# Edge products and one-hot matrices tile by tile in a graph-network kernel

## The chip, the cores and the metric

One core of a Trainium2 chip runs the kernel. The metric is the device time in microseconds (us), the median of several runs. The engines are PE (matrix products; PEld loads its weights), DVE (VectorE), ACT (ScalarE), POOL (GpSimd) and SP, which here only issues DMAs. Data lie in SBUF; PE's results arrive in PSUM.

## The reference

A graph network of three layers over 6250 nodes and 100000 edges, rows of 256 values, three relations. The edges are sorted by their destination. At the end the input is added and each row is normalised.

```python
def _gcn_forward(x, edge_index, edge_type, edge_attr, weights, roots, biases, edge_w, edge_b):
    n = x.shape[0]
    src, dst = (edge_index[0], edge_index[1])
    ew = edge_attr @ edge_w + edge_b
    rel_masks = [(edge_type == i).astype(x.dtype) for i in range(NUM_REL)]
    inv_cnt = [1.0 / jnp.maximum(jax.ops.segment_sum(m, dst, num_segments=n), 1.0) for m in rel_masks]
    for l in range(N_LAYERS):
        residual = x
        msg = jax.nn.relu(x[src] * ew)
        out = jnp.zeros((n, D), dtype=x.dtype)
        for i in range(NUM_REL):
            h = jax.ops.segment_sum(msg * rel_masks[i][:, None], dst, num_segments=n)
            h = h * inv_cnt[i][:, None]
            out = out + h @ weights[l, i]
        out = out + x @ roots[l] + biases[l]
        x = residual + jax.nn.relu(out)
    return x
...
x = _layernorm(x + _L0_gnn_ref(...), axis=-1)
```

## The kernel before

The edges stand in 782 tiles of 128, one edge to a partition, and two tiles make a pair: 391 pairs in each of three layers, 1173 in all. A setup turns the lists of sources, destinations and types into `src_i` (the source row of each edge) and `seg` (for each edge, its relation times 40 plus its destination counted from the first destination of its pair). A window of 40 destinations for each of three relations makes 120 columns (`WK`). During the setup POOL fills the small tile `limits` with hundreds of MEMSETs (L926), and DVE converts integers to floats (L902).

In the order in which the work of one pair depends on itself:

- `gather` (L575): POOL issues two indirect DMAs, one a tile, each of which fetches 128 rows of 256 floats from DRAM into its half of `xs[u]`, by the indices in one column of `src_i`. `xs` has 16 buffers, each of a pair.
- `weigh` (L612): DVE multiplies the pair's rows by the edge weights `ews`, in place. In layer 0 the weights are computed by PE (L589, L602), put into place by ACT (L609) and stored to DRAM; in layers 1 and 2 SP loads them again (L552).
- `bound` (L615): ACT applies the relu.
- `one_hot` (L619): DVE compares a row of the numbers 0 to 119 (`iota_w`) with each edge's `seg`; the result has a 1 in the column of the edge's relation and destination. In layer 0 ACT makes a bf16 copy (L623), from which the edges are counted.
- `reduce` (L629): PE multiplies rows by one-hots, and so adds up the pair's rows by relation and destination into `h_p` (PSUM).
- `add` (L645): DVE adds `h_p` to the window's place in `acc` (SBUF).

When all edges of a block of 128 nodes are in, PE multiplies its sums by the weights (`node_mul`, L673), DVE scales the three results and adds them to the root term (`node_end`, L704 and L705), and the new rows go to `x_mid` in DRAM, from which the next layer gathers; the next layer's first gather thus waits for the last rows. In the last layer ACT and DVE normalise the rows (L710 to L719), the last step by a TENSOR_SCALAR with two scalars a partition.

The order is written out by hand: one loop over steps (L741) issues at step `it` the gather of pair `it + 8`, the reduce of pair `it`, weigh and bound of pair `it + 3`, the add of pair `it - 1` (layer 0) or `it - 3`, what the root term and the nodes need, and last the one-hot of pair `it + 3`. Each engine works through its queue in that order. The two scalars of the change's one-hots and the gathers' indices are columns of `seg` and `src_i`, both in SBUF.

Of the kernel before, what the change touches and what calls it, by code (L numbers as in the profile page):

```python
# [12 lines left out]
ALU = mybir.AluOpType  # L13
# [429 lines left out]
def ordered_path(ctx, tc, x, edge_attr, weights, roots, biases, edge_w, edge_b, out, src_i, seg, place_i, consts):  # L443
# [4 lines left out]
    nc = tc.nc  # L448
    P = 128
# [11 lines left out]
    WK = R * WIN  # L461
# [10 lines left out]
    ident, ones, iota_w = consts  # L472
# [82 lines left out]
    def layer(l, r_sb, b_sb, ews, pools):  # L555
# [11 lines left out]
        xs, ew_ps, ats, ohs, h_ps, turns, o_ps, rs = {}, {}, {}, {}, {}, {}, {}, {}  # L567
# [41 lines left out]
                nc.scalar.activation(ews[q // 2][:, q % 2 * 2 + k], ew_ps[q][:, :, k, :], AF.Copy)  # L609

        def weigh(u):
            nc.vector.tensor_mul(xs[u], ews[u // 4][:, u % 4], xs[u])  # L612

        def bound(u):
            nc.scalar.activation(xs[u], xs[u], AF.Relu)  # L615

        def one_hot(u):
            ohs[u] = edge.tile([P, 2, WK], F32, name="oh", bufs=6)
            nc.vector.tensor_tensor(ohs[u], iota_w[:, None, :].to_broadcast([P, 2, WK]),  # L619
                                    seg[:, 2 * u:2 * u + 2, None].to_broadcast([P, 2, WK]), op=ALU.is_equal)  # L620
            if l == 0:
                oh_bs[u] = edge.tile([P, 2, WK], BF, name="oh_b", bufs=6)
                nc.scalar.activation(oh_bs[u], ohs[u], AF.Copy)  # L623
# [117 lines left out]
        for it in range(-9, max(starts) + 6):  # L741
# [21 lines left out]
            if pair(3) is not None:  # L763
                weigh(pair(3))
                bound(pair(3))
# [32 lines left out]
            if pair(3) is not None:  # L798
                one_hot(pair(3))
# [207 lines left out]
```

## Time and profile before

| | us |
|---|---|
| median of 3 runs | 3129.4 (3127.8 to 3131.9) |
| the profiled execution | 3133.5 |
| its span, first to last instruction | 3131.7 |
| DMA | 668 MB in 295322 packets, 213 GB/s mean |

The chain of work that ended last, by engine, as shares of the span:

```profile
PE 31%; DMA 21%; issue 19%; POOL 17%; DVE 9%; ACT 2%; DVEq 1%; POOLq 0%; ACTq 0%
```

A row of the groups of instructions names the line, the engine, the operation, the tiles, and in the longer form the shapes; then how often it ran, its busy time in us, the mean of one in ns, and the idle time of the engine just ahead of it with what ended it. Busy time of an engine leaves out the issuing of instructions between them. A row of a timeline has the start in us from the span's start, the duration in us, the engine, line, operation and tiles. A row of the windows has the stretch, its length, then busy time and number of instructions of PE, PEld, DVE, ACT and POOL, the granted clock of PE as a share of full speed, the share of time that the DMA engines were busy, and GB/s.

### The profile page before, as it was taken

To read this page: it belongs to the slowest core of one execution; us is meant where nothing else is said; L and a number is where in the kernel's file an instruction comes from. 1 tells how busy PE (TensorE), PEld (TensorE's weight loads), DVE (VectorE), ACT (ScalarE), POOL (GpSimd) and SP (SyncE) were. 2 spreads that over 40 slices of the span, in tenths; PEclk is the share of its full clock that TensorE was granted. 3 is DMA by queue.
4 is the path that set the end of the run, shared out by engine and by line. 5 is a ranking of instruction groups with operands and counts; after the bars stand their busy time and mean duration, and the time that the engine had idled before them with its cause. 6 is when DMAs were issued, how large, how long until landed. Compare 5 with 4: busy or idle time off the path is not lost.

```text
span 3131.7 us, 50860 instructions
## 1 busy us (share of the span) xinstructions
PE 2429.6 (78%) x14938; PEld 2108.6 (67%) x14938; DVE 2003.2 (64%) x4664; ACT 1302.0 (42%) x2524; POOL 2354.9 (75%) x3118
## 2 busy tenths in 40 slices
PE   4898999999998766677777777767677777877765
PEld 3777777778887666666666666656566666666665
DVE  4566666777776455566666666645566677777765
ACT  3666666666776422222333333222223333333332
POOL 7777777777777677777777777767777777777775
PEclk9899899999998778778888888766887888888886
DMA  4777776766776665656666666656666666666664
GB/s 135 233 233 231 222 241 213 228 216 217 230 231 213 217 218 199 213 200 218 205 217 205 221 221 217 206 184 223 211 208 223 220 217 209 224 228 216 218 216 138
DMA packets 295322, 668.14 MB, mean 213 GB/s; under 512 B 147224, under 2 KB 181996, under 8 KB 257788
## 3 DMA queue, kind: packets, MB, share of 16 engines
q1 hardware_dynamic: 175832, 350.27, 32.2%
q0 software_dynamic: 112608, 307.65, 31.6%
q10 hardware_dynamic: 6596, 6.87, 0.6%
q8 instruction: 124, 2.03, 0.3%
q14 instruction: 162, 1.33, 0.1%
HBM read 542.90 MB, written 121.70 MB: 212 GB/s over the span
## 4 chain that ended last, share of the span: by engine, by line
PE 31%; DMA 21%; issue 19%; POOL 17%; DVE 9%; ACT 2%; DVEq 1%; POOLq 0%; ACTq 0%
POOL xs L575 16%; PE h_p L629 15%; DMA xs<-x_mid,src_io 15%; PE o_p L673 7%; DMA xs<-in_x_dram,src_io 6%; PE ew_p L602 4%; DVE x_root L704 3%; DVE xs L612 2%; PE r_p L658 2%; DVE acc L645 2%; PE turn_p L589 1%; ACT ew_s L609 1%; POOL limits L926 1%; DVEq L645 1%; DVE oh L619 1%
## 5 line engine op out<-in xcount | busy, mean ns | idle before, releaser
L575 POOL DMA_INDIRECT xs<-x_mid,src_io x1564 | 1537.5, 983 | 509.0 <-issue 404.6
L629 PE MATMUL h_p<-oh,xs 128*128 128x120 f32 x9384 | 1451.6, 311 | 445.0 <-issue 177.8
L629 PEld LDWEIGHTS h_p<-oh,xs 128*128 128x128 f32 x9384 | 1364.3, 223 | 541.6 <-issue 309.4
L612 DVE TENSOR_TENSOR xs<-ew_s,xs 128x512 f32<-128x512 f32 x1173 | 808.0, 689 | 913.5 <-DMA xs<-x_mid,src_io 566.8
L615 ACT ACTIVATE xs<-xs 128x512 f32<-128x512 f32 x1173 | 739.5, 630 | 1484.9 <-DVE xs L612 1466.3
L575 POOL DMA_INDIRECT xs<-in_x_dram,src_io x782 | 789.6, 1010 | 247.1 <-issue 158.7
L645 DVE TENSOR_TENSOR acc<-h_p,acc 128x240 f32 (+1 forms) x1173 | 519.5, 443 | 147.0 <-PE h_p L629 74.7
L673 PE MATMUL o_p<-w_sb,acc 128*128 128x256 f32 (+1 forms) x1764 | 503.5, 428 | 89.2 <-DVE acc L645 52.1
L619 DVE TENSOR_TENSOR oh<-iota_w,seg_o 128x240 f32<-128x240 f32 x1173 | 467.0, 398 | 0.0
L673 PEld LDWEIGHTS o_p<-w_sb,acc 128*128 128x128 f32 (+1 forms) x1764 | 361.7, 216 | 152.4 <-DVE acc L645 57.6
L658 PE MATMUL r_p<-r_sb,t_s 128*128 128x256 f32 x588 | 216.3, 504 | 79.5 <-ACT t_s L654 78.8
L602 PE MATMUL ew_p<-ew_sb,at 33*128 33x256 f32 x1564 | 235.2, 421 | 10.9 <-ACT at L595 8.8
L609 ACT ACTIVATE ew_s<-ew_p 128x512 f32<-128x512 f32 x391 | 209.4, 587 | 41.5 <-PE ew_p L602 40.5
L704 DVE SCALAR_TENSOR_TENSOR x_root<-o_p,inv,x_root 128x256 f32<-128x256 f32 (+1 forms) x441 | 212.4, 482 | 20.9 <-PE o_p L673 8.6
L623 ACT ACTIVATE oh_b<-oh 128x240 bf16<-128x240 f32 x391 | 160.0, 409 | 117.9 <-DVE oh L619 111.0
L658 PEld LDWEIGHTS r_p<-r_sb,t_s 128*128 128x128 f32 x588 | 130.0, 245 | 111.3 <-ACT t_s L654 95.5
L602 PEld LDWEIGHTS ew_p<-ew_sb,at 33*128 33x128 f32 x1564 | 141.7, 195 | 44.8 <-ACT at L595 16.3
L690 ACT ACTIVATE acc<-zero_o 128x768 f32<-128x768 f32 (+1 forms) x150 | 141.0, 940 | 15.8 <-PE o_p L673 9.2
L629 PE MATMUL h_p<-oh_b,full_ones 128*128 128x120 bf16 x782 | 109.3, 223 | 0.0
L589 PE MATMUL turn_p<-ident_o,an 128*128 128x128 f32 x391 | 89.4, 312 | 7.9 <-DMA an<-in_edge_attr_dram 7.8
L589 PEld LDWEIGHTS turn_p<-ident_o,an 128*128 128x128 f32 x391 | 40.7, 145 | 77.1 <-issue 75.9
L650 PE MATMUL r_p<-ident_o,x_all 128*128 128x128 f32 x294 | 64.1, 303 | 30.9 <-DVE x_root L661 24.8
(84 smaller groups left out, 609.0 us busy)
## 6 DMA issues: line engine op xcount, KB each, us to landing
ew_s<-ew_all SPq DMA_DIRECT2D x194, 1024.0 KB
ew_all<-ew_s SPq DMA_DIRECT2D x97, 1024.0 KB
xs<-x_mid,src_io POOLq DMA_INDIRECT x1564
xs<-in_x_dram,src_io POOLq DMA_INDIRECT x782
an<-in_edge_attr_dram SPq DMA_DIRECT2D x97, 128.0 KB
x_mid<-x_all SPq DMA_DIRECT2D x96, 128.0 KB
x_all<-in_x_dram ACTq DMA_DIRECT2D x8, 768.0 KB
x<-in_x_dram SPq DMA_DIRECT2D x48, 128.0 KB
```

The lines of the kernel that those rows point to most:

```text
L575: nc.gpsimd.indirect_dma_start(out=xs[u][:, i, :], out_offset=None, in_=x_rows[:, :], in_offset=bass.IndirectOffsetOnAxis(ap=src_i[:, t:t ...
L589: nc.tensor.transpose(turns[q][:, k, :], ans[groups.index(q // 2) % 3][:, q % 2 * 2 + k].rearrange("p i a -> p (i a)"), ident)
L602: nc.tensor.matmul(ew_ps[q][:, i, k, :], ats[q][i * UP:i * UP + A1, k, :], ew_sb[i * UP:i * UP + A1, :], start=True, stop=True)
L609: nc.scalar.activation(ews[q // 2][:, q % 2 * 2 + k], ew_ps[q][:, :, k, :], AF.Copy)
L612: nc.vector.tensor_mul(xs[u], ews[u // 4][:, u % 4], xs[u])
L615: nc.scalar.activation(xs[u], xs[u], AF.Relu)
L619: nc.vector.tensor_tensor(ohs[u], iota_w[:, None, :].to_broadcast([P, 2, WK]), seg[:, 2 * u:2 * u + 2, None].to_broadcast([P, 2, WK]), op= ...
L629: nc.tensor.matmul(h_ps[u][:, d, :], xs[u][:, i, d * P:(d + 1) * P] if d < DC else full_ones, (ohs if d < DC else oh_bs)[u][:, i, :], star ...
L645: nc.vector.tensor_tensor(there, h_ps[u][:, :CH].rearrange("p c (r w) -> p c r w", r=R), there, op=ALU.add)
L658: nc.tensor.matmul(rs[c][:, 1, :], t_ss[c][:, d, :], r_sb[:, d, :], start=(d == 0), stop=(d == DC - 1))
L673: nc.tensor.matmul(o_p[:n, r, :], acc[:, d, r, slot:slot + n], w_sb[:, r * DC + d, :], start=(d == 0), stop=(d == DC - 1))
L704: nc.vector.scalar_tensor_tensor(root, o_p[:n, r, :], inv[:n, c, r:r + 1], root, op0=ALU.mult, op1=ALU.add)
```

## The change

The products of a pair, one instruction over both tiles, become one instruction for each tile. The one-hots of a pair, one comparison of two broadcast tensors, become for each tile one comparison of `iota_w` with a scalar for each partition, the edge's entry of `seg`. The order of the loop stays.

```diff
         def weigh(u):
-            nc.vector.tensor_mul(xs[u], ews[u // 4][:, u % 4], xs[u])
+            for i in range(2):
+                nc.vector.tensor_mul(xs[u][:, i, :], ews[u // 4][:, u % 4, i, :], xs[u][:, i, :])
...
         def one_hot(u):
             ohs[u] = edge.tile([P, 2, WK], F32, name="oh", bufs=6)
-            nc.vector.tensor_tensor(ohs[u], iota_w[:, None, :].to_broadcast([P, 2, WK]),
-                                    seg[:, 2 * u:2 * u + 2, None].to_broadcast([P, 2, WK]), op=ALU.is_equal)
+            for i in range(2):
+                nc.vector.tensor_scalar(ohs[u][:, i, :], iota_w, seg[:, 2 * u + i:2 * u + i + 1], None,
+                                        op0=ALU.is_equal)
```

On DVE's queue the first product of a pair now waits for the first tile's gather alone and the second for the second's; the two comparisons follow each other.

## The prediction

> **What bounds the kernel.** The page's first two rows come first: no engine is full.
>
> ```profile
> span 3131.7 us, 50860 instructions
> PE 2429.6 (78%) x14938; PEld 2108.6 (67%) x14938; DVE 2003.2 (64%) x4664; ACT 1302.0 (42%) x2524; POOL 2354.9 (75%) x3118
> ```
>
> POOL's 75% is misleading, as the groups show (busy, mean ns of one, then the idle time ahead of it and who ended it):
>
> ```profile
> L575 POOL DMA_INDIRECT xs<-x_mid,src_io x1564 | 1537.5, 983 | 509.0 <-issue 404.6 <-DMA x_mid<-x_all 32.8 <-PE h_p L629 25.0
> L575 POOL DMA_INDIRECT xs<-in_x_dram,src_io x782 | 789.6, 1010 | 247.1 <-issue 158.7 <-ACT oh_b L623 18.9 <-PE h_p L629 15.8
> L612 DVE TENSOR_TENSOR xs<-ew_s,xs 128x512 f32<-128x512 f32 x1173 | 808.0, 689 | 913.5 <-DMA xs<-x_mid,src_io 566.8
> L619 DVE TENSOR_TENSOR oh<-iota_w,seg_o 128x240 f32<-128x240 f32 x1173 | 467.0, 398 | 0.0
> ```
>
> Taken singly from the trace, the idle time ahead of a gather is 303 to 306 ns, except at the two layer boundaries. So POOL never waits for a buffer: gather follows gather, each at its own duration plus 304 ns. The windows, cut at the first and last gather of each layer, show the same (PE, PEld, DVE, ACT, POOL busy; granted clock; DMA):
>
> ```profile
> 38.30:1066.00 1027.70, 944.78 (x6819) 789.05 (x6819) 687.77 (x1515) 683.63 (x1467) 789.58 (x782) 0.94 0.72 226
> 1066.00:1082.10 16.10, 10.26 (x79) 8.84 (x75) 7.49 (x18) 4.94 (x9) 0.00 (x0) 0.97 0.64 225
> 1082.10:2087.60 1005.50, 719.52 (x3969) 641.55 (x3970) 605.49 (x1410) 296.35 (x493) 767.53 (x782) 0.81 0.63 212
> 2087.60:2104.10 16.50, 11.13 (x43) 9.24 (x41) 6.66 (x16) 2.10 (x3) 0.00 (x0) 0.62 0.12 34
> 2104.10:3112.40 1008.30, 729.85 (x3974) 649.21 (x3974) 674.05 (x1652) 306.74 (x542) 769.97 (x782) 0.80 0.64 215
> 3112.40:3131.70 19.30, 7.50 (x36) 6.43 (x36) 7.50 (x20) 2.29 (x4) 0.00 (x0) 0.76 0.06 18
> ```
>
> The three stages of 782 gathers take 3041.5 us of the span. The shortest gather is 942 ns: 2346 x (0.942 + 0.304) = 2923 us. The rest, 117 us, is gathers that ran longer. The change can only act there, in the three drains (52 us together), or by making another engine late.
>
> **Why gathers run long.** Median 946 ns, but 465 of 2346 take over 1000. The 412 that overlap no DVE instruction average 946, and one of them is long. Of the 465, 464 began while a DVE instruction with two SBUF inputs was running; additions that read PSUM (L645) don't do it. An example from the timeline (start, duration):
>
> ```profile
> 1647.40 0.69 DVE L612 TENSOR_TENSOR xs<-ew_s,xs 128x512 f32<-128x512 f32 x1
> 1647.58 1.33 POOL L575 DMA_INDIRECT xs<-x_mid,src_io  x1 [0.30 <-issue]
> ```
>
> L612 ends 0.51 us after the gather's start, and the gather is 0.39 us longer than 942 ns. Over all cases the excess is (end of the DVE instruction - start of the gather - about 145 ns). With a second such instruction queued right behind, the excess still follows the first one's end (90 cases of L619 before L612): the gather gets in between two instructions. By the instruction in the way, the 117 us are: L612 about 84, L619 22, L705 and others 4, and 7 of a few ns each.
>
> **Part 1, products in halves.** One of 689 ns becomes two of 256 elements; the nearest row is L663 (two SBUF inputs, 128x256), 414 ns. Consecutive DVE instructions overlap by 82 ns in the timeline, so a pair costs DVE 2 x 332 = 664 ns instead of 607: +57. For POOL each half is in the way until its own end alone. The longest excess falls from 689 - 145 = 544 to 414 - 145 = 269 ns, and with starts at random the sum goes with 2 x 269^2 against 544^2, a factor 0.49. Applying the rule to every recorded start of L612, but with two halves there, gives 41 us; moving all starts by -600 to +600 ns gives 41 to 75, mean 56. I take 48, between: **84 - 48 = 36 us saved**. The first half waits for the first gather alone, the second for the second, so the product ends no later.
>
> **Part 2, one-hots by a scalar.** One TENSOR_TENSOR of 240 becomes two TENSOR_SCALARs of 120 elements, one SBUF tensor each. What L619 cost POOL, **22 us**, goes. What a TENSOR_SCALAR costs POOL is the open point.
>
> Duration: L719 is the nearest row (128x256 f32, two scalars read from SBUF), 411 ns at least. Casts of 896 and 784 elements took 630 and 548 ns and one of 391 took 341: some 0.57 ns an element, about half the 1.07 of TENSOR_TENSOR ((689 - 414)/256). At half of 1.07, 120 elements take 411 - 136 x 0.54 = 338, less one scalar (54 ns: L704 with a scalar 482, L705 without 428): 284. At the full 1.07 it would be 265 with both scalars, so the ends lie close. DVE: 2 x (284 - 82) = 404 against 398 - 82 = 316, +88 a pair.
>
> Port: the Trainium skill, "SBUF — State Buffer", section "Who interferes with whom", speaks against this part: TENSOR_SCALAR in its double-rate mode takes the port pair that DVE shares with GpSimd for the whole instruction, and GpSimd, which writes the gathers' descriptors, is fully blocked; TENSOR_TENSOR only keeps GpSimd from reading. Start-up confirms it for POOL's MEMSETs, beside the CAST at 13.4 us and beside the TENSOR_TENSOR at 24.0 (durations min/median/max):
>
> ```profile
> L926 POOL MEMSET limits<- x12: 88/435/569, 13.3 to 13.7; 1x1 f32 x12
> ...
> L926 POOL MEMSET limits<- x17: 88/88/89, 24.0 to 24.5; 1x1 f32 x17
> ```
>
> Beside gathers the 49 L719s show something else: no gather was longer for one, while it was L719 that waited.
>
> ```profile
> 2244.25 0.98 POOL L575 DMA_INDIRECT xs<-x_mid,src_io  x1 [0.30 <-issue]
> 2244.83 0.51 DVE L719 TENSOR_SCALAR x_all<-x_all,mv 128x256 f32<-128x256 f32 x1
> ```
>
> L719s that start 0.49 to 0.60 us into an undelayed gather all end 1.06 us after its start (up to 572 ns instead of 411); those that start at 0.19 to 0.31 us aren't delayed. So a gather uses the pair for a short while some 0.6 to 0.8 us in, and in a shorter one at its start, where L719s beginning 0.1 us ahead lost 10 ns. But no L719 happened to hold the pair at the moment when a gather asked. By those rows a one-hot costs POOL 0. By the rule, it is in the way for all its 284 ns: at the write 284^2 / (2 x 1310 ns, the mean gather period) = 31 ns, at the read (284 - 145)^2 / 2620 = 7.4 ns, together 38 ns x 2346 = 90 us. I take the side of L719, but not its end, since nothing tested the collision: only the last 200 ns hold the pair and half of a delay is absorbed (200^2 / 2620 / 2 = 7.6 ns), plus 2 ns at the read: 9.4 ns x 2346 = **22 us back**.
>
> **Part 3, DVE.** +145 ns a pair; 1173 pairs, 170 us of DVE time, plus its waits for the pair. It hides under POOL: a pair takes POOL about 2.6 us, DVE 1.3 of per-pair work, about 1.45 afterwards, and the last stage's node work adds some 0.35. The 16 xs buffers are the cover: additions come 7 to 9 pairs behind the gathers, 11 at most. If the lag passed 16, every further DVE ns would be paid.
>
> **Drains.** The last products start on landings and the chain then runs through L629, L645, L673 and L704; 0 us, give or take 1 each.
>
> **Sum.** 3133.5 (profiled execution: 3131.7 span and 1.8 around it) - 36 - 22 + 22 = 3097.5. The median of the runs is 4.1 below that execution: **3093 us**, 36 below the median, 1.2%.
>
> **Rivals.**
> - **One-hots cost POOL nothing**: 3133.5 - 58 - 4 = 3071. For it: all 49 L719s. Against: the MEMSETs stalled by a CAST.
> - **One-hots lock GpSimd out (slower)**: the rule in full, 90 us: 3133.5 - 58 + 90 - 4 = 3162. For it: the MEMSET rows, and 2346 such instructions where there were 49. Against: L719s held the pair for much of the first 0.6 us without delaying a gather. It decides once a TENSOR_SCALAR costs POOL over 58/2346 = 25 ns.
> - **DVE becomes late in the last stage**: 674 of 1008 us busy already. If a pair needed 2.7 us there instead of 2.55, 391 x 0.15 = 59 us: about 3152. It needs 0.9 us a pair that I can't find.
>
> **Chances.** Forecast 0.52 (own range 3078 to 3112), one-hots free 0.20, lock-out 0.22, DVE late 0.04; 0.02 for none of these. A measurement of this kernel tells 0.2% (6 us) from no change. Faster: the first two less their upper spill, 0.70; within 0.2%: 0.07; slower 0.23. The range 3058 to 3165 takes in both bounds of the one-hot's price and the lower end of the halves' (41 us).
>
> **What the next profile would show.** Right: L575 still with 304 ns ahead of each, its mean about 977 (992 now over both rows), those that a product holds up at most 1.21 us instead of 1.47; the product's halves at 414; one-hots at 265 to 340. One-hots free: mean near 968. Lock-out: gathers that last until a one-hot's end, mean above 1000. Wrong altogether: POOL idle for a buffer, waiting for PE's L629, or halves that fall on gathers' starts more often than at random.

## The result, and the profile after

| | before | after |
|---|---|---|
| median of 17 runs each, us | 3130.98 (3126.41 to 3138.41) | 3122.41 (3115.45 to 3125.82) |
| ratio, 95% interval | | 0.9971 [0.9964, 0.9979] |
| profiled execution, us | 3133.5 | 3124.6 |
| its span, us | 3131.7 | 3122.8 |

The change makes the kernel 0.3% faster, 9 us. The forecast was 36 us. The page after, its first rows and the shares of the chain:

```profile
span 3122.8 us, 50763 instructions
PE 2404.4 (77%) x14938; PEld 2085.5 (67%) x14938; DVE 2188.1 (70%) x7010; ACT 1306.9 (42%) x2524; POOL 2349.3 (75%) x3118
...
DMA 26%; PE 26%; POOL 15%; issue 15%; DVE 13%; ACT 3%; DVEq 1%; POOLq 0%; ACTq 0%
```

DVE has 185 us more work, and POOL, whose gathers bound the kernel, only 6 us less. The groups (busy, mean ns, idle time ahead and what ended it):

```profile
L575 POOL DMA_INDIRECT xs<-x_mid,src_io x1564 | 1546.1, 989 | 505.6 <-issue 386.5 <-DMA x_mid<-x_all 29.5 <-PE h_p L631 29.0
...
L613 DVE TENSOR_TENSOR xs<-ew_s,xs 128x256 f32<-128x256 f32 x2346 | 910.6, 419 | 713.9 <-DMA xs<-x_mid,src_io 552.8 <-DMA xs<-in_x_dram,src_io 83.2 <-ACT ew_s L609 69.5
L575 POOL DMA_INDIRECT xs<-in_x_dram,src_io x782 | 775.4, 992 | 247.1 <-issue 139.6 <-PE h_p L631 18.9 <-ACT oh_b L625 17.7
...
L621 DVE TENSOR_SCALAR oh<-iota_w,seg_o 128x120 f32<-128x120 f32 x2346 | 588.3, 297 | 0.0
```

Over both gather rows the mean went from 992 to 990 ns, not to 977. In layers 1 and 2 (x_mid) it even rose, from 983 to 989; all of the gain stands in layer 0 (1010 to 992). The windows, cut as before, agree:

```profile
38.45:1050.80 1012.35, 935.43 (x6822) 779.32 (x6823) 746.12 (x2290) 684.74 (x1466) 774.31 (x782) 0.96 0.73 229
1050.80:1067.90 17.10, 9.78 (x74) 8.46 (x72) 8.72 (x25) 5.46 (x10) 1.05 (x1) 0.91 0.62 220
1067.90:2074.10 1006.20, 717.40 (x3966) 637.85 (x3966) 668.04 (x2183) 295.39 (x492) 768.13 (x782) 0.81 0.63 212
2074.10:2088.60 14.50, 8.29 (x44) 7.47 (x44) 8.18 (x25) 2.73 (x4) 1.03 (x2) 0.88 0.17 47
2088.60:3102.70 1014.10, 717.75 (x3972) 640.34 (x3973) 734.28 (x2429) 310.34 (x542) 776.05 (x782) 0.81 0.63 214
```

Layer 0 is 15.3 us shorter, layer 1 as long as before, layer 2 5.8 longer. The books close: the two gather rows hold 5.6 us less busy time and 3.4 us less idle time, the latter at the layer boundaries (29.5 against 32.8 us); that is the 8.9 us of the span.

So what a gather lasts beyond 942 ns is again the whole question: 111.5 us in sum, 117.2 before. Nearly every long gather can be put down to a DVE instruction, since it ends about 0.8 us after the end of the one it waited for: the prediction's 942 - 145 = 797 ns, and in the median some 22 ns more. Of the 465 long ones before, 2 waited beyond the instruction that was running at their start, for the end of a further one. After the change 66 of 498 did. The timeline shows one (start, duration; x2 joins two instructions that follow each other):

```profile
2630.94 0.46 DVE L621 TENSOR_SCALAR oh<-iota_w,seg_o 128x120 f32<-128x120 f32 x2
...
2631.32 0.75 DVE L613 TENSOR_TENSOR xs<-ew_s,xs 128x256 f32<-128x256 f32 x2
2631.49 1.40 POOL L575 DMA_INDIRECT xs<-x_mid,src_io  x1 [0.30 <-issue]
...
2632.31 0.62 DVE L621 TENSOR_SCALAR oh<-iota_w,seg_o 128x120 f32<-128x120 f32 x2
```

The first half of the product began at 2631.32 and, at 419 ns, ended at 2631.74; the second ended at 2632.07. Had the gather got in between, it would have lasted 1.04 us. It lasted 1.40: 2631.49 + 1.40 - 0.797 = 2632.09, the end of the second half. I call this **held through**. The last row is the other side: two one-hots took 0.62 us instead of 0.46 while a gather was 0.8 us into its work.

### The profile page after: what moved, and what is told of

Same layout as the page of the kernel before. It is cut to its first block, busy times and chain, and to the rows that moved or that the text cites. A ratio compares the mean times of both kernels' runs of the same rounds, so it can differ in the third digit from the quotient of the medians.

```text
span 3122.8 us, 50763 instructions
## 1 busy us (share of the span) xinstructions
PE 2404.4 (77%) x14938; PEld 2085.5 (67%) x14938; DVE 2188.1 (70%) x7010; ACT 1306.9 (42%) x2524; POOL 2349.3 (75%) x3118
## 4 chain that ended last, share of the span: by engine, by line
DMA 26%; PE 26%; POOL 15%; issue 15%; DVE 13%; ACT 3%; DVEq 1%; POOLq 0%; ACTq 0%
DMA xs<-x_mid,src_io 22%; POOL xs L575 14%; PE h_p L631 12%; PE o_p L675 7%; DMA xs<-in_x_dram,src_io 5%; DVE xs L613 4%; PE ew_p L602 4%; DVE x_root L706 3%; DVE acc L647 3%; PE r_p L660 2%; DVE oh L621 2%; ACT ew_s L609 1%; PE turn_p L589 1%; POOL limits L928 1%; ACT xs L616 1%
## 5 line engine op out<-in xcount | busy, mean ns | idle before, releaser
L631 PE MATMUL h_p<-oh,xs 128*128 128x120 f32 x9384 | 1434.0, 308 | 436.6 <-DVE acc L647 342.9
L631 PEld LDWEIGHTS h_p<-oh,xs 128*128 128x128 f32 x9384 | 1346.0, 220 | 533.9 <-issue 286.6
L613 DVE TENSOR_TENSOR xs<-ew_s,xs 128x256 f32<-128x256 f32 x2346 | 910.6, 419 | 713.9 <-DMA xs<-x_mid,src_io 552.8
L575 POOL DMA_INDIRECT xs<-in_x_dram,src_io x782 | 775.4, 992 | 247.1 <-issue 139.6
L621 DVE TENSOR_SCALAR oh<-iota_w,seg_o 128x120 f32<-128x120 f32 x2346 | 588.3, 297 | 0.0
L675 PE MATMUL o_p<-w_sb,acc 128*128 128x256 f32 (+1 forms) x1764 | 495.7, 423 | 86.9 <-DVE acc L647 50.3
L602 PE MATMUL ew_p<-ew_sb,at 33*128 33x256 f32 x1564 | 232.4, 417 | 13.0 <-ACT at L595 11.5
L692 ACT ACTIVATE acc<-zero_o 128x768 f32<-128x768 f32 (+1 forms) x150 | 141.0, 940 | 12.6 <-PE o_p L679 6.8
L631 PE MATMUL h_p<-oh_b,full_ones 128*128 128x120 bf16 x782 | 108.2, 221 | 0.0
```

Of the source, the lines that this page charges most:

```text
L575: nc.gpsimd.indirect_dma_start(out=xs[u][:, i, :], out_offset=None, in_=x_rows[:, :], in_offset=bass.IndirectOffsetOnAxis(ap=src_i[:, t:t ...
L602: nc.tensor.matmul(ew_ps[q][:, i, k, :], ats[q][i * UP:i * UP + A1, k, :], ew_sb[i * UP:i * UP + A1, :], start=True, stop=True)
L613: nc.vector.tensor_mul(xs[u][:, i, :], ews[u // 4][:, u % 4, i, :], xs[u][:, i, :])
L621: nc.vector.tensor_scalar(ohs[u][:, i, :], iota_w, seg[:, 2 * u + i:2 * u + i + 1], None, op0=ALU.is_equal)
L631: nc.tensor.matmul(h_ps[u][:, d, :], xs[u][:, i, d * P:(d + 1) * P] if d < DC else full_ones, (ohs if d < DC else oh_bs)[u][:, i, :], star ...
L675: nc.tensor.matmul(o_p[:n, r, :], acc[:, d, r, slot:slot + n], w_sb[:, r * DC + d, :], start=(d == 0), stop=(d == DC - 1))
```

## The experiments

All of them are read in the same sum, by what a long gather waited for. Each row is one profiled execution, in us, with the number of gathers; "others" is every other instruction and a few ns on the rest. A held gather's whole excess stands under "held through", also the part for the first instruction, and also where that was a one-hot. The ratio is to the kernel before on the same chip. Where a layer's code was the same, its excess still scattered by a few us: layer 0 had 53.0 in the kernel before and 50.9 and 58.1 in e11 and e12, and 36.0, 34.5 and 35.0 in e1, e9 and e10.

| kernel | product | held through | one-hot | others | excess | ratio to before, 95% |
|---|---|---|---|---|---|---|
| before | 82.7 (329) | 0.9 (2) | 21.8 (189) | 11.8 | 117.2 | 1 |
| after | 52.9 (390) | 33 (66) | 6.0 (111) | 19.6 | 111.5 | 0.9971 [0.9964, 0.9979] |
| e1 halves alone | 47.0 (423) | 3.4 (6) | 29.4 (268) | 14.9 | 94.7 | 0.9933 [0.9915, 0.9952] |
| e2 one-hots alone | 99.8 (471) | 20.6 (32) | 5.7 (112) | 11.5 | 137.6 | 1.007 [1.005, 1.0089] |
| e3 addition between | 68.8 (528) | 5.6 (11) | 4.4 (80) | 14.4 | 93.2 | 1.0041 [1.0022, 1.006] |
| e4 one-hot between | 79.7 (576) | 5.5 (12) | 6.4 (104) | 12.2 | 103.8 | 0.998 [0.9969, 0.999] |
| e5 TENSOR_TENSOR by tile | 56.1 (394) | 8.2 (15) | 27.6 (291) | 16.3 | 108.2 | 0.9982 [0.9974, 0.9991] |
| e6 the same, whole product | 97.4 (469) | 3.4 (5) | 18.1 (250) | 12.6 | 131.5 | 1.0033 [1.0021, 1.0045] |
| e7 one-hots ahead of addition | 51.0 (374) | 32 (59) | 7.6 (129) | 14.4 | 105.0 | 0.9973 [0.996, 0.9985] |
| e8 quarters | 19.0 (241) | 103 (231) | 11.0 (147) | 15.8 | 148.8 | 1.0133 [1.011, 1.0157] |
| e9 comparison from PSUM | 69.0 (424) | 8.8 (20) | 8.9 | 14.6 | 101.3 | 0.9973 [0.9959, 0.9988] |
| e10 the same from SBUF | 51.6 (378) | 24.2 (48) | 14.9 | 15.0 | 105.7 | 0.9966 [0.9953, 0.9979] |
| e11 e9 with whole product | 109.2 (445) | 1.1 | 7.3 | 12.0 | 129.6 | 1.0058 [1.0046, 1.0071] |
| e12 layers 1, 2 without one-hots | 106.7 (374) | 1.2 | 10.3 | 15.5 | 133.7 | 1.0043 [1.0031, 1.0055] |

### e1 and e2: each part by itself

e1 is the kernel before with the change's `weigh`; e2 is the changed kernel with the product of before.

```diff
 # e1, from before
-            nc.vector.tensor_mul(xs[u], ews[u // 4][:, u % 4], xs[u])
+            for i in range(2):
+                nc.vector.tensor_mul(xs[u][:, i, :], ews[u // 4][:, u % 4, i, :], xs[u][:, i, :])
 # e2, from after
-            for i in range(2):
-                nc.vector.tensor_mul(xs[u][:, i, :], ews[u // 4][:, u % 4, i, :], xs[u][:, i, :])
+            nc.vector.tensor_mul(xs[u], ews[u // 4][:, u % 4], xs[u])
```

> Products in halves, one-hots as before. Theory (gathers that wait behind a first half are often held through the second half too, so that halving saves next to nothing): the gathers' excess over 942 ns each stays at 105 to 117 us in all, 20 us of it from gathers held through both halves; time 3120 to 3131 against 3130 before. Rival (the scalar one-hots take the gain away): without them the 36 us of the prediction show, excess near 81, time near 3094.

> Products whole as before, one-hots by a scalar for each tile. Theory (a one-hot by a scalar costs the gathers about 8 us in all where the whole one-hot cost 22): excess near 103, time near 3116. Rival (the scalar one-hots lock GpSimd out): excess 117 or more, time 3130 or above.

e1 took 3107.4 us against 3127.0 for the kernel before on its chip: **0.9933**, the fastest version of all, faster than the change too. Its gather rows:

```profile
L575 POOL DMA_INDIRECT xs<-x_mid,src_io x1564 | 1532.0, 980 | 507.2 <-issue 376.3 <-DMA x_mid<-x_all 31.3 <-PE h_p L630 29.5
...
L575 POOL DMA_INDIRECT xs<-in_x_dram,src_io x782 | 772.7, 988 | 247.1 <-issue 136.5 <-ACT oh_b L624 21.7 <-PE h_p L630 20.1
```

Against the kernel before these hold 22.4 us less. Halves by themselves are not held through (6 gathers), so the time lies between the two expectations. The one-hot got dearer, 29.4 for 21.8 us (268 gathers for 189): some gathers that no longer met a product may have met a one-hot.

e2 is **slower** than before, 3150.6 us, though its one-hots cost gathers only 5.7 us:

```profile
L575 POOL DMA_INDIRECT xs<-x_mid,src_io x1564 | 1564.1, 1000 | 506.0 <-issue 401.6 <-DMA x_mid<-x_all 30.0 <-DMA xs<-x_mid,src_io 28.0
```

And its timeline (start, duration):

```profile
2466.39 0.47 DVE L620 TENSOR_SCALAR oh<-iota_w,seg_o 128x120 f32<-128x120 f32 x2
...
2466.62 1.66 POOL L575 DMA_INDIRECT xs<-x_mid,src_io  x1 [0.30 <-issue]
2466.77 0.69 DVE L612 TENSOR_TENSOR xs<-ew_s,xs 128x512 f32<-128x512 f32 x1
```

The lock-out of the forecast's slower rival would give gathers that end 797 ns after a one-hot. The timeline shows something else: this gather began during the one-hots, which were over at 2466.86, and lasted until 797 ns after 2467.48, where the product behind them ended (2467.46). Besides 32 such cases, 471 gathers waited for a product, 329 before. So a one-hot alone cost little, but the held gathers, too, had begun during one-hots: with their 20.6 us, one-hots and what followed them held up gathers for 26.3 us, and the plain waits for a product rose by 17.1 us besides.

### e3 and e4: something else between the halves

If a gather is held because the second half follows at once, an instruction that leaves gathers alone, put between, should let it in.

```diff
 # e3, from after: in the loop, ahead of and behind the addition
+                weigh(pair(3), 0)
...
+            if pair(3) is not None:
+                weigh(pair(3), 1)
+                bound(pair(3))
 # e4, from after: in weigh, after each half
+                nc.vector.tensor_scalar(ohs[u][:, i, :], iota_w, seg[:, 2 * u + i:2 * u + i + 1], None,
+                                        op0=ALU.is_equal)
```

> The changed kernel with the addition, which reads PSUM, set between the two halves of a product. Theory (held through both halves): no gather is held through two halves, 20 us go: excess near 90, time near 3101. Rival (the halves only meet more gathers' starts than at random): excess stays near 111, time near 3121.

> The changed kernel with each half of a product followed by one one-hot by a scalar, and the addition after both. Theory (a gather is held over where the next DVE instruction also uses the port pair that DVE shares with GpSimd): fewer gathers pass in between than with the addition, some are held through half, one-hot and half; excess 90 to 115, time 3100 to 3125. Rival (only two products in a row hold on): as with the addition, excess near 90, time near 3101.

Both let it in: 11 and 12 gathers held, for 66. A one-hot by a scalar between the halves thus served as well as the addition, against the theory of e4. But the halves, now apart, met more gathers (528 and 576 for 390), so a part of it came back as plain waits. e4 took 3122.1 us, as long as the change. e3 has the smallest excess of all, 93.2, and was still slower than the kernel before. The waits of POOL say why (us in total, times, longest):

```profile
POOL xs L575 <- issue: 551.6, 1781, 6.2
...
POOL xs L575 <- DMA x_mid<-x_all: 44.0, 2, 30.0
POOL xs L575 <- ACT xs L615: 22.5, 62, 1.7
```

In the changed kernel no wait of a gather is over 0.32 us but at the two layer boundaries. Here gathers waited up to 6.2 us inside layer 0, 17.6 us in all (264.7 idle for 247.1), and 30.0 us at the first boundary, 16.1 in the changed kernel. At the end of each of the nine waits over 0.9 us inside the layers, the reduces stood 14 or 15 pairs behind the gather, so that the pair 16 back had only just been read out of the buffer that the gather wanted; in the changed kernel they stood at most 9 behind. The 16 buffers of `xs` were used up. Around the longest wait:

```profile
767.29 0.53 DVE L646 TENSOR_TENSOR acc<-h_p,acc 128x360 f32 x1 [3.96 <-PE h_p L630]
767.74 0.41 DVE L612 TENSOR_TENSOR xs<-ew_s,xs 128x256 f32<-128x256 f32 x1
767.92 1.05 POOL L575 DMA_INDIRECT xs<-in_x_dram,src_io  x1 [6.15 <-issue]
```

The addition waited 3.96 us for PE, and the second half, which the relu and the next reduce need, came only after it. That this order used up the buffers is likely; it wasn't tested apart.

### e5 to e8: which instructions let a gather be held

```diff
 # e5, from after; e6 the same with the whole product
-                nc.vector.tensor_scalar(ohs[u][:, i, :], iota_w, seg[:, 2 * u + i:2 * u + i + 1], None,
-                                        op0=ALU.is_equal)
+                nc.vector.tensor_tensor(ohs[u][:, i, :], iota_w, seg[:, 2 * u + i:2 * u + i + 1].to_broadcast([P, WK]),
+                                        op=ALU.is_equal)
 # e7, from after: one_hot(pair(3)) moved ahead of add in the loop
 # e8, from e5
-                nc.vector.tensor_mul(xs[u][:, i, :], ews[u // 4][:, u % 4, i, :], xs[u][:, i, :])
+                for h in range(0, D, P):
+                    nc.vector.tensor_mul(xs[u][:, i, h:h + P], ews[u // 4][:, u % 4, i, h:h + P], xs[u][:, i, h:h + P])
```

> The changed kernel, its one-hots tile by tile still, but by a TENSOR_TENSOR with seg broadcast in place of the TENSOR_SCALAR: as many instructions of about the same duration (120 x 1.07 + 139 = 267 ns), without the scalar and without the port pair taken for writing. Theory (it is the TENSOR_SCALARs right ahead of the products behind which gathers are held through a further instruction): 5 or fewer gathers held through where the changed kernel has 64, products cost near 50 us, the one-hots 10 to 15, excess near 70, time 3080 to 3095. Rival (the number of instructions in a row does it, the mode doesn't matter): 40 or more held through, excess near 110, time near 3121.

> Products whole, one-hots tile by tile by TENSOR_TENSOR: against the run with one-hots by a scalar alone it differs in the mode only. Theory (mode): excess near 82 + 13 + 4 = 100, none held through, time near 3112. Rival (count): 30 or more held through a product as in that run, excess near 138, time near 3147.

> The changed kernel with the one-hots of a step moved ahead of its addition, so that an addition stands between the scalar one-hots and the next products. Theory (held through only where products follow the scalar one-hots directly): fewer than 15 gathers held through, excess near 80, time near 3092. Rival (where they stand doesn't matter): 50 or more held through, excess near 111, time near 3121.

> Products in quarters of 128 elements (276 ns each), one-hots tile by tile by TENSOR_TENSOR: the dose of the port rule. Theory (a gather waits for the end of one instruction only): a quarter is in the way for at most 276 - 145 = 131 ns, so products cost 25 us instead of 50, excess near 42, time near 3060. Rival (in a longer row of instructions gathers are held through): excess 80 or more, time 3090 or more.

e5 has the change's instructions in number and place, with TENSOR_TENSOR one-hots of 276 ns. Held gathers fell from 66 to 15, so the operation of the one-hots bears on whether a gather waiting for a product is held. The moment at which a gather starts doesn't explain it: of those that began 165 to 180 ns into a first half that had followed its predecessor at once, 27 of 50 were held in the changed kernel and 2 of 41 in e5. The time didn't fall (3126.2), since these one-hots delay gathers themselves: 27.6 us, not the 10 to 15 expected. e6 has hardly any held ones, yet its products cost 97.4 for 82.7 before and it took 3145.1 us, near its rival's time for another reason. e7 shows that the place of the one-hots isn't what matters: 59 held, and the change's time.

e8 settles that short instructions in a row are no remedy. A quarter of a product takes 287 ns, and the cost of single waits fell to 19 us; but 231 gathers were held, through up to five instructions, and the kernel is 1.3% slower. One of them:

```profile
2479.58 0.47 DVE L622 TENSOR_TENSOR oh<-iota_w,seg_o 128x120 f32<-128x120 f32 x2
2479.66 2.02 POOL L575 DMA_INDIRECT xs<-x_mid,src_io  x1 [0.30 <-PE h_p L632]
...
2479.96 0.90 DVE L614 TENSOR_TENSOR xs<-ew_s,xs 128x128 f32<-128x128 f32 x4
```

The gather began in the first of two one-hots. It ended at 2481.68, and 797 ns before that is 2480.88, the end of the fourth quarter (2480.86).

Counted over the cases in which an instruction with two SBUF inputs stood right behind the one a gather waited for:

| kernel | pair of instructions | held / cases |
|---|---|---|
| before | one-hot, whole product | 1 / 94 |
| e1 | first half, second half | 3 / 173 |
| e5 | the same, TENSOR_TENSOR one-hots by tile | 8 / 145 |
| after | the same, TENSOR_SCALAR one-hots | 59 / 193 |
| e7 | the same | 51 / 160 |
| e2 | TENSOR_SCALAR one-hot, whole product | 26 / 95 |
| e8 | quarters | 115 / 285 |

One thing is common to all held ones behind a first half or quarter. Where DVE had idled before that first instruction, none was held: 0 of 319 over the kernels after, e1, e5, e7, e8, e9 and e10. Where it had followed its predecessor at once, 59 of 151 were in the changed kernel and 3 of 141 in e1. So an unbroken row of instructions goes with it, but isn't enough. Whether the gather or the next instruction gets the turn at the end of an instruction, and what decides it, isn't settled by these runs.

### e9 and e10: the one-hots' reading of SBUF

Layers 1 and 2 compare from a copy of `iota_w` in PSUM (e9) or from SBUF (e10); layer 0 keeps the one-hots of before. Both have the PSUM copy and four `h_p` buffers, so they differ in one operand.

```diff
+            iota_p = iota_pool.tile([P, WK], F32, name="iota_p")
+            nc.scalar.activation(iota_p, iota_w, AF.Copy)
...
+                    nc.vector.tensor_scalar(ohs[u][:, i, :], iota_p, seg[:, 2 * u + i:2 * u + i + 1], None,
+                                            op0=ALU.is_equal)
```

> Products in halves. Layer 0: the one-hot of a pair whole, as before. Layers 1 and 2: one-hots tile by tile by a scalar, with the numbers 0 to 119 read from PSUM instead of SBUF (four buffers for h_p instead of five, to make room). A TENSOR_SCALAR that reads PSUM leaves the shared port pair alone, if the theory of the port is right: in layers 1 and 2 no gather waits for a one-hot and fewer than 8 are held through a further product, so their excess falls from 59 us (halves with whole one-hots) to 30 to 45, with layer 0 at 36; time 3085 to 3098. Rival (scalar one-hots of any source bring it about, by their number and place): 30 or more held through in layers 1 and 2, excess there 65 or more, time 3115 or more.

> The same kernel, four h_p buffers too, with the numbers in SBUF: differs from the run beside it in the source alone. Theory: in layers 1 and 2 as the changed kernel, 30 or more gathers held through further products, excess there near 73, with layer 0 at 36 a time near 3118. Rival (the source doesn't matter): the same time as the run with PSUM.

From PSUM a one-hot takes 333 ns instead of 299 and delayed no gather at all; from SBUF 86 gathers, 4.6 us together. In layers 1 and 2 held gathers fell from 47 (23.6 us) to 19 (8.4 us). But the product's plain waits rose: 49.7 us there for 32.1. The excess of the two layers is 66.8 us in e9 and 70.7 in e10, and the times are the same, 3119.7 and 3119.1 us: the theory was right about the one-hots' waits, but asked for fewer than 8 held ones, and the time is that of its rival.

### e11 and e12: the whole product beside one-hots that delay nothing

In e2, e4, e6 and e9 the product became dearer when something else became cheaper. A theory for it: in the kernel before, a gather that starts during the whole one-hot of 398 ns waits, gets in at its end, and so stands ahead of the 689 ns product. The one-hot was a shield; take it away, and the gather starts in the product, at a higher price. e11 is e9 with the whole product, and thus has four `h_p` buffers where the kernel before has five. e12 is the kernel before without any one-hot in layers 1 and 2; a tile of zeros stands for them.

```diff
 # e12, from before
+            if l > 0:
+                ohs[u] = oh_none
+                return
```

> Products whole. Layers 1 and 2: one-hots by a scalar with the numbers read from PSUM, which delayed no gather in the run with halves; layer 0 as before; four h_p buffers. Before, the gathers of layers 1 and 2 lost 64 us, 12 of it behind one-hots. Theory (a whole one-hot ahead of a product shields it: a gather that waits behind the one-hot gets in at its end, and one that doesn't is met by the product): the 12 us go, but products meet gathers more often, 46 us become 60 or more; excess in layers 1 and 2 60 to 80, time 3125 to 3150. Rival (costs add up): 64 - 12 = 52 us, time near 3115.

> The kernel before with the one-hots of layers 1 and 2 left out: the products with rows take a tile of zeros instead, so these layers add nothing to the nodes' sums. Theory (shield): with no one-hots at all products meet gathers more often than the 26% before, excess in layers 1 and 2 60 to 80, time 3125 to 3145 although 782 DVE instructions are gone. Rival (costs add up): the 12 us behind one-hots go and nothing comes, excess 52 there, time near 3115.

The gathers of layers 1 and 2 in e11, and of e12, with a one-hot that delays nothing and with none:

```profile
L580 POOL DMA_INDIRECT xs<-x_mid,src_io x1564 | 1552.0, 992 | 505.9 <-issue 404.3 <-DMA x_mid<-x_all 30.0 <-DMA xs<-x_mid,src_io 25.9
...
L629 DVE TENSOR_SCALAR oh<-iota_p,seg_o 128x120 f32<-128x120 f32 x1564 | 453.5, 330 | 0.0
```

```profile
L577 POOL DMA_INDIRECT xs<-x_mid,src_io x1564 | 1548.9, 990 | 509.3 <-issue 407.2 <-DMA x_mid<-x_all 33.2 <-DMA xs<-x_mid,src_io 27.7
```

The kernel before has 983 there. Its one-hots delayed gathers by 12 us in these layers; without that delay the excess of the two layers *rose*, from 64.2 to 78.7 and 75.6 us, and the product's share from 45.5 to 72.6 and 67.2. Both kernels are slower than before, one of them with 467 - 156 = 311 us less work on DVE. Where a one-hot could shield a product is where the product began right behind another DVE instruction. Counted in layers 1 and 2:

| kernel | products right behind another: delay, mean of one | products after idle time of DVE: delay, mean of one |
|---|---|---|
| before | 23.8 us in 445, 53 ns | 22.4 us in 337, 66 ns |
| e11 | 50.1 us in 481, 104 ns | 23.6 us in 301, 78 ns |
| e12 | 35.2 us in 357, 99 ns | 32.8 us in 425, 77 ns |

By the prediction's formula a whole product met at random would cost 544^2 / 2620 = 113 ns (an estimate). Before, a product behind a one-hot cost half of that; without the shield it costs nearly all of it. In e11 almost the whole rise is there. In e12 about half of it is in products that began after idle time, of which there are more, so the shield is not all of that rise. Both runs lie in the theory's range of excess; e12's time, 3146.4 us, is just above its 3145. In its profiled execution some 2 us more than before are at the boundaries and the tail and 5 in layer 0, whose code is unchanged.

## Why the prediction was wrong

Its sum and what came of it, in us of excess, each class as the forecast had left it:

| | forecast | measured | difference |
|---|---|---|---|
| product, waiting for one instruction | 48 | 52.9 | +4.9 |
| held through a further one | 0 | 33 | +33 |
| one-hots | 22 | 6.0 | -16 |
| others | 11 | 19.6 | +8.6 |
| boundaries | 0 | -3.3 | -3.3 |

The differences come to +27: 9 us gained instead of 36.

- **The step that failed** is in the part on why gathers run long: "the gather gets in between two instructions". It was counted on a one-hot ahead of a whole product (1 held of 94 on recount) and then used for two halves behind TENSOR_SCALARs, a sequence that the trace of before doesn't hold. There it failed in 59 of 193. Of the 33 us of the held gathers some 10 are the wait for the first instruction, which the 48 was meant to hold; about 23 is what being held cost. e1, e5, e7 and e8 show that it isn't a property of halves, but of what else is in the kernel and of how many short instructions stand in a row.
- **The sum itself failed second.** Part 1 and Part 2 were costed alone and added. By excess, e1 alone saved 22.5, e2 alone lost 20.4, and both together saved 5.7: near the sum of the two runs, but not of the forecast, because Part 2's "22 us goes" left out who was behind the one-hot. With whole products, gathers that no one-hot delays meet the product instead (e11, and in part e12). With halves, the plain waits and the 10 us of the held ones come to 63 us for the 48 forecast, where e1 with its whole one-hots has 47: that is the second term, some 15 us. Against the two, 23 and 15, and 9 us of others, stand 16 us less at the one-hots and 3 at the boundaries.
- **Part 1, the halves, was right by itself.** Forecast 48 us left; in e1 47.0, and 3.4 held. A half took 422 ns there, 414 forecast. That 48 came so near is in part luck: it was chosen between the 41 of the replayed starts and the 56 of shifted ones. Even so the span gained less than 36, since e1's one-hots and others took back 10.7.
- **Part 2, the price of a TENSOR_SCALAR, was right in kind.** The trace's L719 against the rule of the Trainium skill ("SBUF — State Buffer", section "Who interferes with whom"): the row won. In the write's stretch no gather was delayed by a one-hot; those that ran when a gather began and weren't followed by a hold delayed it by 99 ns at most, 6.0 us in all, where the rule in full would have been 90 (the prediction's estimate). Five of the held gathers began in a one-hot, too, and were held through the product behind it. The 22 taken was too much; the lock-out rival fell, although e2 came near it with 3150.6 us, for another reason. The duration was some 272 ns where nothing interfered, 284 forecast, and 297 in the mean, with up to 532 beside gathers. The forecast's 54 ns for a scalar came from L704 and L705, which differ in more than that: L704 also reads `o_p` from PSUM.
- **Part 3 was right.** DVE's 185 us (170 forecast) hid: ahead of gathers stand 303 to 306 ns as before. That the cover of 16 buffers can end was seen in e3. The rival of a late DVE fell for the change itself.
- **The drains** came 3.3 us shorter, forecast 0 give or take 1 each.
- Of the signs, the mean gather (977 forecast, 990 found) and the longest product delay (1.21 us; held ones last 1.44 us in the mean, 0.942 + 33/66) were the two that told it. "Halves that fall on gathers' starts more often than at random" was named as what would make it wrong, but the 63 us lie within the 41 to 75 of the prediction's own shifted starts. The halves fell on gathers' starts about as at random; the 48 had counted on less.

**Open:** what decides whether a gather gets in at the end of an instruction. One-hots by TENSOR_SCALAR from SBUF and unbroken rows of short instructions go with it (47 for 19 held in e10 and e9; 231 in e8), but no run isolates it.

## What to carry to other kernels

When one engine's work runs long because another's instructions are in its way, don't cost those instructions one by one: a block that is taken away can let the victim run into the next one, and that may be the dearer. Look first at what stands right behind it in the queue, and test each part of a change alone; here one half of the change, by itself, gained 20 us where the whole gained 9. A long instruction that is cut into pieces which follow each other at once is not shorter for the one that waits, unless the trace shows that it gets in between.

## What the runs showed of the hardware

- A gather waiting behind DVE can be held through several instructions that follow each other, five further ones and 2.02 us in the example of e8 instead of 0.94; with a one-hot ahead of a whole product, in the kernel before, this was 1 case of 94. Behind a first half or quarter that began after idle time of DVE it was 0 of 319.
- A TENSOR_SCALAR that reads PSUM delays no gather (e9: 0; e11: 0), and takes 330 to 333 ns for 120 elements where one from SBUF takes 297 to 299 in the changed kernel and e10.
- Beside gathers it is mostly the TENSOR_SCALAR from SBUF that waits: one-hots running 0.6 to 0.8 us into a gather took up to 532 ns instead of some 272. To such a one-hot alone a gather of the changed kernel lost 99 ns at most.
- With less work on DVE the gathers were slower: e12 has no one-hot in two layers, and 11.4 us more excess there.
